# Token norms as a broadcast subtraction on VectorE and a broadcast product on GpSimd, and strided copies turned to strided reads

## The chip, the cores and the metric

The kernel runs on one core of a Trainium2 chip. A core has five engines that work side by side, each through its own instruction list in order: TensorE (PE, with its weight loads shown as PEld), VectorE (DVE), ScalarE (ACT), GpSimd (POOL) and SyncE (SP, which issues most DMAs). Matrix products are written to PSUM, a small memory of eight banks of 512 floats per partition; everything else lies in SBUF. GpSimd works on SBUF here, the other engines on both. The metric is the device time of one execution in microseconds (us). One execution was also recorded by the hardware profiler; all views below are of it.

## The reference

Two "metaformer" layers over x of shape [16, 128, 32, 32] (16 samples, 128 channels, 1024 positions, called tokens). Cut to what matters:

```python
# layer 0
x = x + linear_attention(layernorm_over_channels(x, eps=1e-6))   # group norm, q/k/v, softmaxes
t = tokens(x)                                                    # [16, 1024, 128]
t = t + stu(layernorm(t, eps=1e-5))                              # FFT convolution with 16 filters, 3 taps
x = image(t)
# layer 1
x = x + conv_block(layernorm_over_channels(x, eps=1e-6))         # 3x3 conv, bn, relu, 3x3 conv, bn, + , relu
t = tokens(x)
t = t + experts(layernorm(t, eps=1e-5))                          # 64 experts choose 8 tokens each of a sample
x = image(t)
```

Each of the four norms takes every token by itself: the mean and the variance over its 128 channels, then `(v - m) / sqrt(s + eps)`. These are the token norms of the title: 4 per sample, 64 in all.

## The kernel before

A sample is held as [128 channels x 1024 tokens], in eight tiles of 128 tokens (`NT = 8`). For a norm it is turned by eight transposes on PE (`transpose_in`, L128, or `transpose_in_classes`, L133, which takes the tokens q, q+8, q+16, ... as class q) into a PSUM tile `big` of two banks, [128 tokens x 8 x 128 channels]. ACT copies the tile to SBUF (`tok` L312, `ub` L416, `tok` L760, `tt` L791). `token_stats` reads PSUM: eight `bn_stats` (L95), then small operations on [128 x 8] (L99 to L105) on DVE that give the mean m, the sum q and the variance a (L103), and `rsqrt`, five small operations on POOL (L85 to L89), which gives r. The norm itself is done in eight pieces, one for each tile: in stage A by ACT (`token_norm_act`, L120, with the small helper nm = -m*r on DVE, L118), in stage C by DVE (`token_norm`, L111). Each piece is turned back by a transpose on PE (`transpose_out`, L138) into another `big`.

The stages, with the times of the profiled execution:

- A, 0 to about 487 us, `attention(b)` for 16 samples. The norm of `tok`; gt (L319 to L321), pg (L325, PE) and ga (L327, then rsqrt on POOL) for the group norm; xn (L335); the keys: matmul (L342), maximum ks (L349), broadcast subtraction ke (L350, DVE, PSUM to SBUF), exponential (L353, ACT), sum and reciprocal (L365, L366), broadcast product (L367, POOL, in place); the queries: matmul (L360), maximum (L362, DVE), exponential (L364, ACT), transposes (L128) and copy qt (L376), L377 and L378; the context cx (L385, L389), wy (L394, copied in L396), wt (L400, copied in L402); output py (L408) and the sum into x (L409). Then the norm of `ub`, the transposed copy u (L426), the spectra (matmuls L436 for two parities, values by L221 to L234, "butterflies" L252 to L268, POOL for the even parity and DVE for the odd one), the three-tap products (L453), their sum into x (L459) and its store (L460). `filters()` runs beside it: it loads 16 tiles mi (L469) and mixes them on DVE (L473, L475), and computes the spectra ph of the filters.
- G, about 487 to 787 us: filters made and multiplied (L528 to L590; copies with strided reads L541 and L543, contiguous ones L580 and L582). Nothing is changed here.
- C, about 787 to 1576 us, `convolve_and_route(b)`: inverse spectra (`classes`, on POOL and DVE, L701 to L728; matmul L749), sum into x (L754), norm of `tok`, copy into a padded image (L767), two convolutions (L666, 18 matmuls for each half), ACT and DVE between them (L771, L778, L781), sum into x (L783, POOL), norm of `tt`, transposes, copy tk (L799), gate product (L808), and for every second sample the choice of tokens (up to gt, L826), transposes of gt (L128, copy gtt L834) and the pooling pp (L840, copied in L845 and L849).
- the experts and the final sum, about 1576 to 1737 us. Nothing is changed here.

Samples overlap: `interleave` holds up to five samples of A (a new one every 4 steps) or four of C as generators, and at every `yield` goes on to the next one. A scheduling framework then orders the instructions of each engine and puts in the waits; each engine's order is fixed in the program. Tiles come from rings: `big` has three buffers in stage A and two in stage C, `tok` has three in A. A buffer is free again only when its last reader is done. So in A the centre of a loop is the chain L103 (DVE), rsqrt (POOL), norm, L138 (PE), and the two norms of different samples share DVE, POOL and the ring.

The strided copies: `ub` holds tokens by class, and `u` shall hold them in order. L426 read PSUM straight and wrote SBUF with a step of eight elements; L754 likewise wrote x, read and written with that step:

```python
nc.scalar.copy(
    u.rearrange("p (s q) -> p q s", q=NQ), pu.rearrange("p (q s) -> p q s", q=NQ)
)
```

The functions that the diff touches, with the line numbers of the profile:

Of the kernel before, what the change touches and what calls it, by code (L numbers as in the profile page):

```python
# [8 lines left out]
F32 = mybir.dt.float32  # L9
AF = mybir.ActivationFunctionType  # L10
ALU = mybir.AluOpType
# [3 lines left out]
P = 128  # L15
B, C, H, W = 16, 128, 32, 32
N = H * W
NT = N // 128
# [12 lines left out]
NQ = 8  # L31
# [24 lines left out]
def metaformer_kernel(ctx: ExitStack, tc: tile.TileContext, io: dict, out: bass.AP):  # L56
    nc = tc.nc
# [24 lines left out]
    def rsqrt(r, a, t):  # L82

        g = nc.gpsimd
        g.tensor_tensor(r, a, mhalf[:, : a.shape[1]], ALU.pow)  # L85
        g.tensor_tensor(t, r, r, ALU.mult)
        g.tensor_tensor(t, t, a, ALU.mult)
        g.tensor_scalar(t, t, -0.5, 1.5, ALU.mult, ALU.add)
        g.tensor_tensor(r, r, t, ALU.mult)  # L89

    def token_stats(work, src, eps):

        bst = work.tile([P, NT, 6], F32, name="bst", tag="bst")
        for j in range(NT):
            nc.vector.bn_stats(bst[:, j, :], src[:, j, :])  # L95
        sts = work.tile([P, 6, NT], F32, name="sts", tag="sts")
        m, q, r, d, a, t = (sts[:, i, :] for i in range(6))
        me, qe, mo, qo = (bst[:, :, i] for i in (1, 2, 4, 5))
        nc.vector.tensor_tensor(d, me, mo, ALU.subtract)  # L99
        nc.vector.tensor_tensor(q, qe, qo, ALU.add)  # L100
        nc.vector.tensor_tensor(d, d, d, ALU.mult)
        nc.vector.scalar_tensor_tensor(q, d, C / 4.0, q, ALU.mult, ALU.add)
        nc.vector.tensor_scalar(a, q, 1.0 / C, eps, ALU.mult, ALU.add)  # L103
        nc.vector.tensor_tensor(m, me, mo, ALU.add)
        nc.vector.tensor_scalar(m, m, 0.5, None, ALU.mult)  # L105
        rsqrt(r, a, t)
        return m, q, r

    def token_norm(dst, src, m, r):
        for j in range(NT):  # L110
            nc.vector.tensor_scalar(  # L111
                dst[:, j, :], src[:, j, :], m[:, j : j + 1], r[:, j : j + 1],
                ALU.subtract, ALU.mult,
            )

    def token_norm_act(work, dst, src, m, r):
        nm = work.tile([P, NT], F32, name="nm", tag="nm")
        nc.vector.scalar_tensor_tensor(nm, m, -1.0, r, ALU.mult, ALU.mult)  # L118
        for j in range(NT):
            nc.scalar.activation(  # L120
                dst[:, j, :], src[:, j, :], AF.Identity,
                bias=nm[:, j : j + 1], scale=r[:, j : j + 1],
            )

    def transpose_in(pt, src):

# [33 lines left out]
    with ExitStack() as l0:  # L160
# [42 lines left out]
        with ExitStack() as a0:  # L203
# [3 lines left out]
            work = a0.enter_context(tc.tile_pool(name="awork", bufs=2))  # L207
# [81 lines left out]
            for h in range(HEADS):  # L289
                s = slice(h * DH, (h + 1) * DH)  # L290
# [11 lines left out]
            def big():  # L302
                return ps.tile([P, N], F32, name="big", tag="big", bufs=3)

            def attention(b):
                if b + 2 < B:
                    load(b + 2)
                xb = xt[b]
                pt = big().rearrange("p (j c) -> p j c", c=C)
                transpose_in(pt, xb)  # L310
                tok = work.tile([P, NT, C], F32, name="tok", tag="tok", bufs=3)
                nc.scalar.copy(tok, pt)  # L312
                m, q, r = token_stats(work, pt, 1e-6)

                yield
                token_norm_act(work, tok, tok, m, r)

                gt = work.tile([P, NT + 1], F32, name="gt", tag="gt")
                nc.vector.scalar_tensor_tensor(gt[:, :NT], q, 1.0 / C, r, ALU.mult, ALU.mult)  # L319
# [12 lines left out]
                px = big()  # L332
# [40 lines left out]
                pt = big().rearrange("p (j c) -> p j c", c=C)  # L373
# [19 lines left out]
                pw = ps.tile([P, P], F32, name="pw", tag="s")  # L393
                nc.tensor.matmul(pw, cx, wout, start=True, stop=True)  # L394
                wy = work.tile([P, P], F32, name="wy", tag="wy")
                nc.vector.tensor_copy(wy, pw)  # L396

                yield
                pw = ps.tile([P, P], F32, name="pw", tag="s")
                nc.tensor.matmul(pw, wv, wy, start=True, stop=True)  # L400
                wt = work.tile([P, P], F32, name="wt", tag="wt")
                nc.vector.tensor_copy(wt, pw)  # L402

                yield
                py = big()
                for hf in range(2):
# [6 lines left out]
                pt = big().rearrange("p (j c) -> p j c", c=C)  # L413
                transpose_in_classes(pt, xb)
                ub = work.tile([P, NT, C], F32, name="ub", tag="ub")
                nc.scalar.copy(ub, pt)  # L416
                m, q, r = token_stats(work, pt, 1e-5)

                yield
                token_norm_act(work, ub, ub, m, r)  # L420

                yield
                pu = big()
                transpose_out(pu, ub)
                u = work.tile([P, N], F32, name="u", tag="u")
                nc.scalar.copy(  # L426
                    u.rearrange("p (s q) -> p q s", q=NQ), pu.rearrange("p (q s) -> p q s", q=NQ)
                )

                yield  # L430
# [31 lines left out]
            def filters():  # L462
# [34 lines left out]
                nc.vector.tensor_tensor(ph[:, :, half:], e, o, ALU.subtract)  # L497

            interleave(attention, 5, 4, filters())


# [114 lines left out]
    with ExitStack() as c1:  # L616
        cconst = c1.enter_context(tc.tile_pool(name="cconst", bufs=1))
        work = c1.enter_context(tc.tile_pool(name="cwork", bufs=2))
# [34 lines left out]
        for n in range(2):  # L653
            for i in range(2):
                pt = cconst.tile([P, HP, HP], F32, name=f"pad{n}{i}", tag=f"pad{n}{i}")
# [20 lines left out]
        def tokens(t):  # L676
            return t.rearrange("p (j c) -> p j c", c=C)
# [58 lines left out]
        def convolve_and_route(b):  # L736
            pr, j = divmod(b, 2)
# [4 lines left out]
            xb = xt[b]  # L742
# [3 lines left out]
            px = big()  # L746
            for q in range(NQ):
                for r in range(2):
# [1 line left out]
                        px[:, q * P : (q + 1) * P], z[:, q, r, :], wi[:, q, r, :],  # L750
                        start=(r == 0), stop=(r == 1),
                    )
            xv = xb.rearrange("p (s q) -> p q s", q=NQ)
            nc.vector.tensor_tensor(xv, px.rearrange("p (q s) -> p q s", q=NQ), xv, ALU.add)  # L754
            yield

            pt = tokens(big())
            transpose_in(pt, xb)
            tok = work.tile([P, NT, C], F32, name="tok", tag="tok")
            nc.scalar.copy(tok, pt)  # L760
            m, q, r = token_stats(work, pt, 1e-6)
            yield
            token_norm(tok, tok, m, r)
            yield
            px = big()
            transpose_out(px, tok)
# [8 lines left out]
            for hf in range(2):  # L775
                pc = conv(p2, cw[1], hf)
                r = work.tile([P, 16, W], F32, name="r", tag="r")
# [9 lines left out]
            pt = tokens(big())  # L787
            transpose_in(pt, xb)
            tt = work.tile([P, NT, C], F32, name="tt", tag="tt", bufs=4)
            toks[b] = tt  # L790
            nc.scalar.copy(tt, pt)  # L791
            m, q, r = token_stats(work, pt, 1e-5)
            yield
            token_norm(tt, tt, m, r)
            yield
            pu = big()
            transpose_out(pu, tt)
# [53 lines left out]
            )  # L851

        interleave(convolve_and_route, 4, 4)


# [5 lines left out]
    with ExitStack() as e1:  # L861
        work = e1.enter_context(tc.tile_pool(name="ework", bufs=2))
# [153 lines left out]
```

## Time and profile before

| what | us |
|---|---|
| three runs, median (lowest to highest) | 1737.72 (1735.78 to 1739.06) |
| the profiled execution | 1738.64 |
| its span | 1736.7 |
| PE busy, DVE busy | 1464.6, 883.2 |
| ACT busy, POOL busy | 583.6, 634.6 |
| rsqrt's first step on POOL, L85, 64 times | 108.6 |
| norm by ACT in stage A, L120, 256 pieces | 102.0 |
| norm by DVE in stage C, L111, 256 pieces | 68.4 |
| four kinds of ACT copies, 64 in all | 64.8 |
| u by L426, x by L754, 16 each | 32.2, 32.7 |

In the profile a group of instructions is written as line, engine, operation, output<-inputs by the program's names, and how many; then busy time in all, mean ns of one, and after the bar the idle time of that engine just before them, with what ended it. In a row of PE's waits, `PE big L138 <- DVE tt L111` is a transpose that stood until DVE had made tt; the numbers are us in total, times, and the longest. The chain of waits goes back from the last instruction: each piece is released by the one before it. L12 is line 12 of the kernel before.

### The profile page before, as it was taken

To read this page: it belongs to the slowest core of one execution; us is meant where nothing else is said; L and a number is where in the kernel's file an instruction comes from. 1 tells how busy PE (TensorE), PEld (TensorE's weight loads), DVE (VectorE), ACT (ScalarE), POOL (GpSimd) and SP (SyncE) were. 2 spreads that over 40 slices of the span, in tenths; PEclk is the share of its full clock that TensorE was granted. 3 is DMA by queue.
4 is the path that set the end of the run, shared out by engine and by line. 5 is a ranking of instruction groups with operands and counts; after the bars stand their busy time and mean duration, and the time that the engine had idled before them with its cause. 6 is when DMAs were issued, how large, how long until landed. Compare 5 with 4: busy or idle time off the path is not lost.

```text
span 1736.7 us, 32853 instructions
## 1 busy us (share of the span) xinstructions
PE 1464.6 (84%) x13704; PEld 943.4 (54%) x13704; DVE 883.2 (51%) x2509; ACT 583.6 (34%) x919; POOL 634.6 (37%) x926
## 2 busy tenths in 40 slices
PE   3688888888789999973999989999799979965675
PEld 2566666666568888862455444554455445432232
DVE  5676777767456666655345443533545253411114
ACT  3456655666345555540112221212112121211000
POOL 2354433444257777763333222331333133110000
PEclk9899999999889999995999989999899989986677
DMA  6311211211234444448101010110101000007965
GB/s 229 111 70 64 85 74 74 85 74 62 85 111 119 131 124 125 122 145 289 41 25 37 25 37 25 32 29 13 49 25 37 1 13 1 12 0 267 393 246 208
DMA packets 136420, 160.29 MB, mean 92 GB/s; under 512 B 4944, under 2 KB 104400, under 8 KB 133840
## 3 DMA queue, kind: packets, MB, share of 16 engines
q1 hardware_dynamic: 135504, 156.10, 26.4%
q8 instruction: 107, 1.75, 0.4%
q0 software_dynamic: 768, 2.10, 0.3%
q14 instruction: 41, 0.34, 0.1%
HBM read 102.61 MB, written 55.57 MB: 91 GB/s over the span
## 4 chain that ended last, share of the span: by engine, by line
PE 55%; DVE 14%; issue 11%; POOL 10%; ACT 4%; DMA 4%; SPq 2%; DVEq 0%; POOLq 0%; ACTq 0%
PE pcv L666 23%; PE pg L534 8%; PE py L554 8%; POOL sts L85 4%; PE big L749 3%; PE big L138 2%; DVE bst L95 2%; PE big L436 2%; PE big L128 2%; POOL ke L367 1%; POOL x L783 1%; PE pp L840 1%; PE big L808 1%; PE big L453 1%; ACT ub L120 1%
## 5 line engine op out<-in xcount | busy, mean ns | idle before, releaser
L666 PE MATMUL pcv<-pad,cw 128*128 128x512 f32 x1152 | 507.3, 595 | 0.7 <-ACT pad L767 0.7
L666 PEld LDWEIGHTS pcv<-pad,cw 128*128 128x128 f32 x1152 | 214.0, 190 | 259.6 <-issue 258.2
L85 POOL TENSOR_TENSOR sts<-sts,mhalf 128x8 f32<-128x8 f32 x64 | 108.6, 1697 | 296.5 <-DVE sts L103 296.5
L541 DVE COPY g<-pg 128x512 f32<-128x512 f32 x256 | 164.9, 686 | 97.4 <-PE pg L534 94.0
L543 ACT COPY g<-pg 128x512 f32<-128x512 f32 x256 | 137.5, 589 | 127.4 <-PE pg L534 118.9
L534 PE MATMUL pg<-ph,mst 32*128 32x128 f32 x4096 | 155.6, 287 | 6.1 <-ACT g L543 4.7
L95 DVE BATCH_NORM_STATS2 bst<-big 128x6 f32<-128x128 f32 x512 | 111.0, 280 | 77.4 <-ACT tt L791 61.4
L534 PEld LDWEIGHTS pg<-ph,mst 32*128 32x128 f32 x4096 | 131.0, 190 | 32.3 <-issue 25.2
L554 PE MATMUL py<-g,v 128*32 128x128 f32 x4096 | 140.3, 276 | 3.0 <-issue 2.3
L783 POOL TENSOR_TENSOR x<-x,r 128x512 f32<-128x512 f32 x32 | 40.5, 1265 | 258.7 <-ACT r L781 258.7
L554 PEld LDWEIGHTS py<-g,v 128*32 128x32 f32 x4096 | 105.5, 109 | 20.1 <-issue 5.4
L771 ACT ACTIVATE pad<-pcv,bn 128x512 f32<-128x512 f32 x32 | 25.0, 781 | 262.8 <-PE pcv L666 262.8
L523 POOL TENSOR_TENSOR v<-xc 128x512 f32<-128x512 f32 x64 | 80.6, 1287 | 47.1 <-PE py L554 29.6
L778 DVE SCALAR_TENSOR_TENSOR r<-pcv,bn,pad 128x512 f32<-128x512 f32 x32 | 24.0, 751 | 137.2 <-PE pcv L666 136.4
L453 PE MATMUL big<-u,mu 128*128 128x128 f32 (+4 forms) x384 | 92.2, 381 | 1.2 <-ACT u L426 1.2
L128 PE MATMUL big<-ident,x 128*128 128x128 f32 x384 | 56.7, 285 | 42.5 <-POOL x L783 23.0
L749 PE MATMUL big<-wi,z 128*128 128x128 f32 x512 | 70.3, 296 | 23.5 <-POOL z L703 21.2
L749 PEld LDWEIGHTS big<-wi,z 128*128 128x128 f32 x512 | 68.1, 211 | 29.9 <-POOL z L703 21.5
L436 PE MATMUL big<-wf,ub 128*128 128x256 f32 x256 | 67.4, 404 | 13.7 <-ACT u L426 7.8
L128 PEld LDWEIGHTS big<-ident,x 128*128 128x128 f32 x384 | 46.0, 146 | 55.6 <-POOL x L783 27.4
L781 ACT ACTIVATE r<-r,bn 128x512 f32<-128x512 f32 x32 | 23.1, 722 | 144.2 <-DVE r L778 144.0
L138 PE MATMUL big<-ident,tok 128*128 128x128 f32 x256 | 42.0, 299 | 34.3 <-DVE tok L111 17.9
(210 smaller groups left out, 2313.7 us busy)
## 6 DMA issues: line engine op xcount, KB each, us to landing
vd<-xf SPq DMA_DIRECT2D x16, 1024.0 KB, 3.8
xc<-vd SPq DMA_DIRECT2D x16, 1024.0 KB, 6.7
yd<-ys SPq DMA_DIRECT2D x32, 512.0 KB, 4.2
y<-yd SPq DMA_DIRECT2D x32, 512.0 KB, 5.5
w1t<-in_weight SPq DMA_DIRECT2D x16, 1024.0 KB, 14.7
w2t<-in_weight SPq DMA_DIRECT2D x16, 1024.0 KB, 14.4
x<-in_x SPq DMA_DIRECT2D x16, 512.0 KB, 3.5
mi<-in_M_phi SPq DMA_DIRECT2D x16, 512.0 KB, 3.9
```

The source lines that it names most:

```text
L85: g.tensor_tensor(r, a, mhalf[:, : a.shape[1]], ALU.pow)
L95: nc.vector.bn_stats(bst[:, j, :], src[:, j, :])
L128: nc.tensor.transpose(pt[:, j, :], src[:, j * P : (j + 1) * P], ident)
L436: lambda q, dst: nc.tensor.matmul(dst, ub[:, q, :], wf[:, q, :], start=True, stop=True),
L453: nc.tensor.matmul(pa[:, a:hi], mu[:, NF - 1 - si, tap, :], u[:, a - tap : hi - tap], start=(tap == 0), stop=(tap == KU - 1),)
L523: nc.gpsimd.tensor_tensor(vv[:, x, 1 + r], xc[:, :, 0, :, r, :], xc[:, :, 1, :, r, :], op)
L534: nc.tensor.matmul(pg[r][:, i], mst[rs, 4 * q + i, :], ph[rs, c, :], start=True, stop=True,)
L541: nc.vector.tensor_copy(dst, src)
L543: nc.scalar.copy(dst, src)
L554: nc.tensor.matmul(py[rows, x, kl, :], v[:, (x * NM + m) * JL + jl, 1 - ri : 3 - ri, :] .rearrange("p k b -> p (k b)"), g[:, ((x * NM + m) ...
L666: nc.tensor.matmul(pc, wt[:, tap, :], src[:, hf * 16 + dy : hf * 16 + dy + 16, dx : dx + W], start=(tap == 0), stop=(tap == 8),)
L749: nc.tensor.matmul(px[:, q * P : (q + 1) * P], z[:, q, r, :], wi[:, q, r, :], start=(r == 0), stop=(r == 1),)
```

## The change

The norm is split otherwise. `token_center` is one DVE operation on the whole tile: it reads PSUM, subtracts the mean (broadcast over the channels) and writes SBUF. It takes the place of ACT's copy and needs no r, and stands right behind `token_stats`. `token_scale` is one POOL operation, in place in SBUF, which multiplies by r (broadcast). It stands where the eight pieces stood; nm is gone. The copies of wy and wt go from DVE to ACT. The copies u and the sum L754 write SBUF in order and read PSUM with the step.

```diff
-    def token_norm(dst, src, m, r):
-        for j in range(NT):
-            nc.vector.tensor_scalar(
-                dst[:, j, :], src[:, j, :], m[:, j : j + 1], r[:, j : j + 1],
-                ALU.subtract, ALU.mult,
-            )
-
-    def token_norm_act(work, dst, src, m, r):
-        nm = work.tile([P, NT], F32, name="nm", tag="nm")
-        nc.vector.scalar_tensor_tensor(nm, m, -1.0, r, ALU.mult, ALU.mult)
-        for j in range(NT):
-            nc.scalar.activation(
-                dst[:, j, :], src[:, j, :], AF.Identity,
-                bias=nm[:, j : j + 1], scale=r[:, j : j + 1],
-            )
+    def token_center(dst, src, m):
+        nc.vector.tensor_tensor(
+            dst, src, m.unsqueeze(2).to_broadcast([P, NT, C]), ALU.subtract
+        )
+
+    def token_scale(dst, r):
+        nc.gpsimd.tensor_tensor(dst, dst, r.unsqueeze(2).to_broadcast([P, NT, C]), ALU.mult)
...
                 tok = work.tile([P, NT, C], F32, name="tok", tag="tok", bufs=3)
-                nc.scalar.copy(tok, pt)
                 m, q, r = token_stats(work, pt, 1e-6)
-
-                yield
-                token_norm_act(work, tok, tok, m, r)
+                token_center(tok, pt, m)
+
+                yield
+                token_scale(tok, r)
...
-                nc.vector.tensor_copy(wy, pw)
+                nc.scalar.copy(wy, pw)
...
-                nc.vector.tensor_copy(wt, pw)
+                nc.scalar.copy(wt, pw)
...
                 ub = work.tile([P, NT, C], F32, name="ub", tag="ub")
-                nc.scalar.copy(ub, pt)
                 m, q, r = token_stats(work, pt, 1e-5)
-
-                yield
-                token_norm_act(work, ub, ub, m, r)
+                token_center(ub, pt, m)
+
+                yield
+                token_scale(ub, r)
...
                 nc.scalar.copy(
-                    u.rearrange("p (s q) -> p q s", q=NQ), pu.rearrange("p (q s) -> p q s", q=NQ)
+                    u.rearrange("p (s q) -> p s q", q=NQ), pu.rearrange("p (q s) -> p s q", q=NQ)
                 )
...
-            xv = xb.rearrange("p (s q) -> p q s", q=NQ)
-            nc.vector.tensor_tensor(xv, px.rearrange("p (q s) -> p q s", q=NQ), xv, ALU.add)
+            xv = xb.rearrange("p (s q) -> p s q", q=NQ)
+            nc.vector.tensor_tensor(xv, px.rearrange("p (q s) -> p s q", q=NQ), xv, ALU.add)
...
             tok = work.tile([P, NT, C], F32, name="tok", tag="tok")
-            nc.scalar.copy(tok, pt)
             m, q, r = token_stats(work, pt, 1e-6)
-            yield
-            token_norm(tok, tok, m, r)
+            token_center(tok, pt, m)
+            yield
+            token_scale(tok, r)
...
-            nc.scalar.copy(tt, pt)
             m, q, r = token_stats(work, pt, 1e-5)
-            yield
-            token_norm(tt, tt, m, r)
+            token_center(tt, pt, m)
+            yield
+            token_scale(tt, r)
```

## The prediction

> **What bounds the kernel now.** I read the page first: no engine is full over the whole span, so the share of busy time decides nothing, and each stage has to be read for itself.
>
> ```profile
> span 1736.7 us, 32853 instructions
> PE 1464.6 (84%) x13704; PEld 943.4 (54%) x13704; DVE 883.2 (51%) x2509; ACT 583.6 (34%) x919; POOL 634.6 (37%) x926
> ```
>
> The change touches stage A (0 to 487 us) and stage C (787 to 1576 us). One steady sample of A, in the table by windows, takes 25.45 us (the distance of two L409):
>
> ```profile
> 311.93:337.38 25.45, 22.41 (x127) 16.51 (x127) 18.64 (x62) 16.35 (x29) 11.59 (x23) 1.00 0.21 84
> ```
>
> The columns after the length are PE, its weight loads, DVE, ACT and POOL. PE lacks 3 us, DVE 6.8, POOL 13.9: no engine sets the pace. The chain of waits in the same stretch shows what does, a loop through DVE, POOL and back:
>
> ```profile
> 322.60 0.17 DVE sts L103
> ...
> 322.89 1.66 POOL sts L85
> ...
> 325.96 0.89 ACT ub L120 x2
> ...
> 329.68 1.91 POOL ke L367
> 331.59 1.61 POOL sts L85
> ...
> 334.11 0.21 POOL sts L89
> ...
> 336.02 1.28 DVE x L409
> ```
>
> The reader should see that POOL is on the chain although it is idle more than half of the time. In stage C, PE is full with the convolution (L666) but for three stretches where one group of samples ends and the next begins; the waits of PE in that stage (total us, times, longest) name them:
>
> ```profile
> PE big L128 <- POOL x L783: 23.0, 15, 2.5
> PE big L138 <- DVE tt L111: 19.5, 4, 7.0
> PE big L138 <- DVE tok L111: 17.9, 4, 10.5
> PE big L128 <- issue: 9.0, 3, 3.0
> ```
>
> **The prices.** From the groups of instructions:
>
> ```profile
> L350 DVE TENSOR_TENSOR ke<-big,ks 128x1024 f32<-128x1024 f32 x16 | 19.4, 1212 | 0.0
> L367 POOL TENSOR_TENSOR ke<-ke,ks 128x1024 f32<-128x1024 f32 x16 | 31.0, 1939 | 71.4 <-PE big L138 36.1 <-DVE sts L103 20.5 <-DVE qs L377 12.7
> L120 ACT ACTIVATE ub<-ub,nm,sts 128x128 f32<-128x128 f32 x128 | 51.0, 480 | 35.4 <-DVE nm L118 35.4
> L111 DVE TENSOR_SCALAR tok<-tok,sts 128x128 f32<-128x128 f32 x128 | 34.2, 340 | 43.4 <-POOL sts L89 43.4
> L426 ACT COPY u<-big 128x1024 f32<-128x1024 f32 x16 | 32.2, 2010 | 9.2 <-PE big L138 9.2
> L754 DVE TENSOR_TENSOR x<-big,x 128x1024 f32<-128x1024 f32 x16 | 32.7, 2043 | 70.4 <-PE big L749 70.4
> L799 ACT COPY tk<-big 128x1024 f32<-128x1024 f32 x16 | 16.2, 1014 | 31.4 <-PE big L138 31.1
> L95 DVE BATCH_NORM_STATS2 bst<-big 128x6 f32<-128x128 f32 x512 | 111.0, 280 | 77.4 <-ACT tt L791 61.4
> ```
>
> Centre: L350 is the same operation in form (PSUM in, SBUF out, small factor broadcast): 1.21 us. Scale: L367 likewise, 1.91 as median and 2.36 at worst, when DVE worked beside it; I take 1.95. The old norm was eight pieces, 3.19 us on ACT or 2.14 on DVE, the first done after 0.5 or 0.36; the new scale releases all eight transposes (L138) together. Copies of the strided u (L426) and sum (L754) keep the strided side, but read it from PSUM. No row strides over two PSUM banks; within one bank the strided reads L541 and L543 (686 and 589 ns) equal the contiguous L580 and L582 (681 and 586). So u is between 1.01 (L799) and 2.01, L754 between 1.21 and 2.04, and I take the lower values, the nearest rows.
>
> [...]
>
> **Stage A, steady.** Removed per sample: two ACT copies (L312, L416, 1.01 each), 16 activations (L120), two nm (L118), two DVE copies that go to ACT (L396, L402, 0.28 each; about the same there, on an engine with 9 us to spare, so they cost nothing; if ACT were late they would add 0.3 each ahead of L400 and L408). Added: two centres (2.4 on DVE), two scales (3.9 on POOL). ACT falls to some 9 us, DVE rises by 1.5 to about 20, POOL to 15.5. All still fit in 25.4. The loop does not stay, because order changes on two engines:
>
> - On DVE the centre of ub stands ahead of L103, whose output POOL waits for. Before, L103 ended at 322.76; now at 323.87.
> - On POOL: rsqrt (2.9) to 326.8, scale of ub (1.95) to 328.75, L367 to 330.7, rsqrt of tok (2.8) to 333.5. Before it was 334.32: from L103 the leg is 9.63 instead of 11.56, since the tok statistics no longer queue on DVE behind L118. L367 is not later than its other input, L366, allows.
> - After that rsqrt, DVE executes L319 to L321 (0.45) and only then L362, the maximum of q (1.2), in 10 of 16 samples; before, L362 stood ahead of the wait and was over by 331.7. Then L364 on ACT (1.3), L408 (1.9; its PSUM buffer is the one that L364 reads), L409 (1.3): end 339.75. This leg is 6.25 instead of 3.0. Behind L362 on DVE wait L459, L377 and L409.
> - From L409 to the next L103: 10.9 before. The centre adds 1.2, the copies and nm take 0.25 away, and L436's odd half starts some 0.55 before L409's end instead of 0.06 behind it (its buffer comes free with L234): 11.25.
>
> Sum 9.63 + 6.25 + 11.25 = 27.1; with the PE stalls before L138 (328.75 against 326.5 for the first piece before), partly made good by u's missing 1.0 us, I take 27.0 to 27.3, +1.7 per sample. On PE, L325 (for ga) now comes after all eight transposes of tok instead of among them: nothing, since xn (L335) needs those transposes as well. On SP's queue two loads of mi (L469) come earlier, between loads of x; each 512 KB load lands in about 4 us and DMA engines are 21% busy here: nothing, and 4 us once if a load of x stood behind them. Bounds: if what stands behind L362 is not late, 26.4 (+1.0), less what PE's slack takes back (+0.6); with matmul ends as listed 28.1 (+2.7). About ten such periods lie between 118 and 412 us: **+17** (+6 to +28).
>
> Fill (0 to 118 us): xn of the first sample waits for the ga chain, which the change does not shorten: 0 (-3 to +3).
>
> Drain (412 to 487 us): here samples no longer overlap. In the last one L103 goes ahead of the centre. Before, rsqrt ended 470.52, the eight pieces and transposes ran to 476.3, u was copied until 478.75. Now the scale ends at 472.8, eight transposes in a row at 475.0 (0.27 each at that place), u at 476.05: -2.7. Two samples before it gain about 0.7 each by u: **-4** (-6 to 0; 0 with u at 2.01).
>
> **Stage C.** Per sample go two ACT copies and 16 L111, and come two centres and two scales. PE is full in most of it, so DVE's and POOL's new work is covered by L666 (7.7 us per 18 matmuls); POOL's L783 wait shows what it costs if the scale falls ahead of L783: up to 1.95 a time. I price that at nothing since L783 is ready when L781 is, a few us after the scales.
>
> At the three boundaries: L95 of tt waits for no copy (-1.0), L754 is 0.8 shorter, and the tok statistics no longer stand behind L111 and L845, which waited for 31 matmuls (L840, to 1042.66). Their L103 falls at about 1037.75 instead of 1043.43; rsqrt to 1041.4 (behind the scale of tt, POOL first), scale to 1043.4, transposes from 1043.5 to 1045.2, pad and first L666 at about 1046.5 where it was 1051.63; less 0.6 for L749 that now follow in one block: -4.5 each, **-13.5** (-18 to -4). Start of C: one copy and L754 less, a centre and an unsplit scale more: 0 (-1 to +1). In the steady part, at some four places a transpose of the next tile needs the PSUM buffer that the centre now holds 0.85 longer than the copy did: **+3.5** (0 to +7). End of C: centre ahead of L103 and the eight cold transposes behind the scale, one copy less: **+1.5** (0 to +3).
>
> Sum: +17 - 4 - 13.5 + 3.5 + 1.5 = +4.5. The profiled execution took 1738.64 us (span 1736.7 and 1.9 around it), 0.9 above the median of the three runs, 1737.72. So about 1742.
>
> **Rivals.**
> 1. *The loop of A is not stretched, faster.* If L362's delay is taken by the depth of five samples in flight (PSUM ring of three buffers, PE with 3 us of slack) and the removed copies free DVE early, A adds at most 0.6 a sample: +6 - 4 - 13.5 + 3.5 + 1.5 = -6.5; with no stretch at all -12.5. Time 1725 to 1732. Against it: the order of DVE puts L362 behind a wait for POOL. It decides where the period stays under 26.2.
> 2. *POOL sets the pace, much slower.* POOL works 15.5 of 25.4 us, all of it in the chain. With scale and L367 at 2.36, and L252 to L257 (the spectra's even half) queued between them, the period goes to 28 and over: +27, boundaries then only -3 each: +20, about 1758.
> 3. *The strided read costs what the strided write did.* u and L754 stay at 2.0: drain 0, boundaries -3.7 each, period +0.5 more: about +15, 1753. The change then only moves the stride. The contiguous-equal rows L541 and L580 speak against it.
>
> **How the numbers follow.** Forecast 0.43 (its own range 1734 to 1751), rival 1 0.32, rival 2 0.17, rival 3 0.08. Within 0.2% (3.5 us, about what a measurement of this kernel can tell from no change) lie 0.13 of the forecast's chance and 0.03 of rival 1; below it 0.04 and 0.29; the rest above. Faster 0.33, same 0.16, slower 0.51. The range reaches to 1722 (rival 1 with the boundaries' full bound) and 1764 (rival 2 with the contention at its worst row), leaving out about 0.2.
>
> **What would show it.** Right: windows between L409 of 27 us in steady A; PE waiting for POOL's scale before L138; L362 behind L319 with ACT waiting at L364; boundaries of C 4 us shorter; u near 1.0 and L754 near 1.2. Wrong: a steady window of 25.5 or less (rival 1), a scale over 2.3 with DVE beside it (rival 2), u at 2.0 (rival 3). The sum is most exposed to the number of stretched periods, and to PE's order, where eight L138 in a row now wait at one place with L453 and L436 behind them.

## The result and the profile after

The changed kernel takes 1789.43 us (median of 4 runs, 1785.93 to 1791.74) against 1737.73 us of the kernel before beside it: 1.0297 times, 95% interval 1.0275 to 1.0318. That is 2.97% slower, 51.7 us, where +4 was forecast and the range ended at 1764. In the profiled execution the span is 1786.2 us, 49.5 more than before. The page of the changed kernel:

```profile
span 1786.2 us, 32455 instructions
PE 1467.9 (82%) x13704; PEld 952.3 (53%) x13704; DVE 895.0 (50%) x2253; ACT 414.9 (23%) x631; POOL 750.3 (42%) x990
```

ACT lost 169 us of work, POOL gained 116, DVE 12, and PE has the same work. In the changed kernel the line numbers are 8 lower from stage A on (L401 is the old L409, L354 the old L362, L400 the old L408, L445 the old L453, L658 the old L666); L110 is the centre, L115 the scale, L130 the transposes L138. Where the 49.5 us lie, from the first and last instruction of one line in each stage:

| stretch | before | after | difference | forecast |
|---|---|---|---|---|
| A, fill: to the third sum of py into x (L409, now L401) | 118.2 | 127.7 | +9.5 | 0 |
| A, steady: from the third to the fourteenth | 294.1 | 337.7 | +43.6 | +17 |
| A, drain: to the first product of G | 73.4 | 74.2 | +0.8 | -4 |
| G: its first to its last pg | 277.9 | 279.2 | +1.3 | 0 |
| start of C: to the first convolution product | 57.0 | 57.9 | +0.9 | 0 |
| C: first to last convolution product | 721.7 | 712.5 | -9.2 | -13.5 + 3.5 |
| the rest | 194.4 | 197.0 | +2.6 | +1.5 |

Stage C came out nearly as forecast. Stage A is the miss, and within it the steady part: one sample takes 30.7 us instead of 25.4. The table by windows (as in the prediction: length, then PE, weight loads, DVE, ACT, POOL, granted clock, DMA) of one steady sample, and below it three parts of the same sample:

```profile
374.64:405.32 30.68, 23.31 (x127) 17.21 (x127) 22.36 (x61) 7.69 (x12) 15.15 (x25) 0.94 0.18 68
385.50:395.80 10.30, 8.18 (x37) 5.27 (x38) 6.86 (x21) 2.07 (x2) 8.65 (x12) 1.00 0.01 2
395.80:400.40 4.60, 1.84 (x9) 1.28 (x7) 4.36 (x5) 1.22 (x3) 1.92 (x2) 0.98 0.00 0
400.44:404.00 3.56, 3.56 (x6) 1.56 (x7) 1.58 (x4) 0.42 (x1) 2.33 (x5) 0.55 0.41 158
```

No engine is full here either, but two things are new. From 395.8 to 400.4 PE works only 1.84 us of 4.6 while DVE is busy, and in the stretch behind it PE's granted clock is 0.55. The timeline of this sample (start, us, engine, line, operation; in brackets the idle time before it and what ended it) names both, and the delay of L99 before them:

```profile
388.27 1.20 DVE L357 TENSOR_REDUCE ks<-ke 128x32 f32<-128x1024 f32 x1
388.58 1.90 POOL L115 TENSOR_TENSOR ub<-ub,sts 128x1024 f32<-128x1024 f32 x1
389.39 1.11 DVE L99 TENSOR_TENSOR sts<-bst 128x8 f32<-128x8 f32 x1
...
395.90 1.90 POOL L115 TENSOR_TENSOR tok<-tok,sts 128x1024 f32<-128x1024 f32 x1
396.06 1.76 DVE L312 TENSOR_TENSOR gt<-gt,sts 128x8 f32<-128x8 f32 x1
397.86 0.16 DVE L313 TENSOR_REDUCE gt<-gt 128x1 f32<-128x8 f32 x1
397.93 1.21 DVE L354 TENSOR_REDUCE qs<-big 128x1 f32<-128x1024 f32 x1
...
400.44 3.56 PE L400 MATMUL big<-xn,wt 128*128 128x512 f32 x4 [2.80 <-ACT qe L356]
```

In the steady sample of the kernel before, L312 (there L320) and L400 (there L408) read:

```profile
333.53 1.88 PE L408 MATMUL big<-xn,wt 128*128 128x512 f32 x4
335.64 0.15 DVE L320 TENSOR_TENSOR gt<-gt,sts 128x8 f32<-128x8 f32 x1
```

L312 works on 128x8 numbers and took 0.155 us on average before. Now it takes 1.76 in ten of the 16 samples, this one among them, and ends at 397.82, just after POOL's scale of tok (395.90 + 1.90 = 397.80). L99 ends at 390.50, just after the scale of ub (390.48). Neither shows idle time before it: the delay hides as length. Then L354, L356 and L400 follow late, PE has stood 2.80 us, and four products that took 1.88 before, at a granted clock of 1.00, take 3.56 at 0.55.

### The profile page after: what moved, and what is told of

Same layout as the page of the kernel before. It is cut to its first block, busy times and chain, and to the rows that moved or that the text cites. A ratio compares the mean times of both kernels' runs of the same rounds, so it can differ in the third digit from the quotient of the medians.

```text
span 1786.2 us, 32455 instructions
## 1 busy us (share of the span) xinstructions
PE 1467.9 (82%) x13704; PEld 952.3 (53%) x13704; DVE 895.0 (50%) x2253; ACT 414.9 (23%) x631; POOL 750.3 (42%) x990
## 3 DMA queue, kind: packets, MB, share of 16 engines
q1 hardware_dynamic: 135504, 156.10, 25.6%
## 4 chain that ended last, share of the span: by engine, by line
PE 58%; DVE 13%; issue 11%; POOL 10%; DMA 4%; ACT 3%; SPq 1%; DVEq 0%; POOLq 0%; ACTq 0%
PE pcv L658 23%; PE pg L526 8%; PE py L546 7%; PE big L741 3%; POOL sts L85 2%; PE big L130 2%; PE big L120 2%; PE big L400 2%; DVE bst L95 2%; PE big L428 2%; PE big L334 2%; PE big L800 1%; POOL ke L359 1%; POOL x L775 1%; PE pc L377 1%
## 5 line engine op out<-in xcount | busy, mean ns | idle before, releaser
L658 PE MATMUL pcv<-pad,cw 128*128 128x512 f32 x1152 | 506.5, 594 | 0.7 <-ACT pad L759 0.7
L658 PEld LDWEIGHTS pcv<-pad,cw 128*128 128x128 f32 x1152 | 213.3, 189 | 259.2 <-issue 258.1
L445 PE MATMUL big<-u,mu 128*128 128x128 f32 (+4 forms) x384 | 95.0, 394 | 16.5 <-DVE ub L110 16.5
L741 PE MATMUL big<-wi,z 128*128 128x128 f32 x512 | 64.9, 285 | 24.3 <-POOL z L695 21.8
L741 PEld LDWEIGHTS big<-wi,z 128*128 128x128 f32 x512 | 63.2, 200 | 31.3 <-POOL z L695 22.0
L445 PEld LDWEIGHTS big<-u,mu 128*128 128x128 f32 x384 | 57.1, 195 | 35.9 <-DVE ub L110 18.7
L746 DVE TENSOR_TENSOR x<-big,x 128x1024 f32<-128x1024 f32 x16 | 19.6, 1225 | 111.0 <-PE big L741 110.7
L120 PEld LDWEIGHTS big<-ident,x 128*128 128x128 f32 x384 | 45.1, 145 | 50.2 <-POOL x L775 27.5
L896 POOL DMA_DIRECT2D ed<-og x16 | 8.7, 546 | 137.7 <-DVE og L895 137.7
```

What stands on the lines that cost most here:

```text
L120: nc.tensor.transpose(pt[:, j, :], src[:, j * P : (j + 1) * P], ident)
L445: nc.tensor.matmul(pa[:, a:hi], mu[:, NF - 1 - si, tap, :], u[:, a - tap : hi - tap], start=(tap == 0), stop=(tap == KU - 1),)
L658: nc.tensor.matmul(pc, wt[:, tap, :], src[:, hf * 16 + dy : hf * 16 + dy + 16, dx : dx + W], start=(tap == 0), stop=(tap == 8),)
L741: nc.tensor.matmul(px[:, q * P : (q + 1) * P], z[:, q, r, :], wi[:, q, r, :], start=(r == 0), stop=(r == 1),)
```

## Theories and experiments

Theory 1: DVE operations on SBUF alone stand while POOL's scale runs; L312 delays L354, and PE's idle time then halves its clock. Rival 2: POOL's chain of rsqrt, scale and product sets the period, and L312 only lies beside it. Rival 3: L312 is slow because it shares the operand r with the scale. Later a fourth came in: a second loop through the centre and the scale of ub. (These rivals are not those of the prediction.) Each run below is given as its median time and its ratio to the kernel before, run beside it, with the 95% interval.

**The delayed operation: its kind.** First L312 with one tensor input:

```diff
-nc.vector.scalar_tensor_tensor(gt[:, :NT], q, 1.0 / C, r, ALU.mult, ALU.mult)
-nc.vector.tensor_tensor(gt[:, :NT], gt[:, :NT], r, ALU.mult)
+nc.vector.tensor_scalar(gt[:, :NT], r, 1.0 / C, None, ALU.mult)
+nc.vector.tensor_scalar(gt[:, :NT], gt[:, :NT], 1.0, None, ALU.mult)
```

> The changed kernel; L311 and L312 on DVE become operations with one tensor input (r, then gt), at the same place in every engine's order and with the same wait for r; what they compute (the weight of a token in the group norm) is left out. Theory 1 (DVE operations with two SBUF inputs stand while POOL works on its scale): L312 falls from 1.76 to about 0.16 us though it still reads while the scale runs, and PE's idle time before L400 shrinks by 1.6 us; if PE's lowered clock at L400 (0.55 granted) follows from that idle time, L400 x4 falls from 3.56 to 1.9 as well. A steady period goes from 30.7 to 29.1 without and 27.4 with the clock's part; times 11 that is 1772 or 1753 us. Rival 2 (POOL's chain of rsqrt, scale, product sets the period, L312 is only beside it): 1789, unchanged. Rival 3 (L312 is slow because it shares the operand r with the scale): L312 stays at 1.76, 1789.

Measured: 1786.64 us, 1.0291 (1.026 to 1.0322), steady period 30.7. The timeline of this kernel:

```profile
393.98 1.90 POOL L115 TENSOR_TENSOR tok<-tok,sts 128x1024 f32<-128x1024 f32 x1
394.14 1.76 DVE L312 TENSOR_SCALAR gt<-gt 128x8 f32<-128x8 f32 x1
```

L312 stands as long as before, now with one input and without r. So rival 3 falls, and theory 1 in the form "two inputs" as well. Taken alone, the unchanged time would have spoken for rival 2; that L312 was not relieved shows that the run had not tested it. The next run changes the kind of operation only:

```diff
-nc.vector.tensor_tensor(gt[:, :NT], gt[:, :NT], r, ALU.mult)
+nc.vector.tensor_reduce(gt[:, :NT], gt[:, :NT].unsqueeze(2), AX.X, ALU.add)
```

> The changed kernel; only L312 on DVE becomes a reduction over one element (output as input; the second factor r of the group norm's weight is left out), at the same place in every engine's order, still behind the same wait for r. In the run with a one-input TENSOR_SCALAR at L312 it stayed at 1.76 us and the time at 1787. Theory 1a (what is kept from running beside POOL's product is the kind of DVE operation: two SBUF inputs or a copy-like one from SBUF to SBUF, but not a reduction): L312 takes 0.16, a steady period falls from 30.7 to 29.1, and to 27.4 if PE's low clock at L400 came from the idle time that L312 causes; times 11: 1771 or 1753 us. Rival (any small SBUF operation of DVE stands while POOL's scale runs, or the period is set elsewhere): L312 1.76 or the time at 1787.

Measured: 1760.26 us, 1.012 (1.0103 to 1.0136): 29 us of the 52 are gone by the kind of one operation on 1024 numbers in each sample, at the same place in the order and behind the same waits. Its timeline and the window of L400:

```profile
379.39 1.90 POOL L115 TENSOR_TENSOR tok<-tok,sts 128x1024 f32<-128x1024 f32 x1
379.54 0.16 DVE L312 TENSOR_REDUCE gt<-gt 128x8 f32<-128x8 f32 x1
...
382.32 1.98 PE L400 MATMUL big<-xn,wt 128*128 128x512 f32 x4 [1.19 <-ACT qe L356]
```

```profile
382.32:384.30 1.98, 1.98 (x6) 0.97 (x7) 1.59 (x4) 0.42 (x1) 0.75 (x2) 1.00 0.64 265
```

The reduction runs beside the scale in 0.16 us, PE stands 1.19 us instead of 2.80, keeps its clock (1.00), and the steady period is 27.5. Theory 1a holds: 1.6 us of delay and 1.6 us of clock in each of the eight samples where PE had stood 2.8 us make 25.6, and A ends 26.8 us earlier (512.8 instead of 539.6).

By kind, beside the scale's 1.90 us: 1.76 us for the TENSOR_TENSOR, with two inputs, 1.76 for the TENSOR_SCALAR, with one, and 0.16 for the reduction. What ties the delay to the instruction's kind no run here shows; "locked" and "lock" in the expectations below are the author's words for an operation that stands like this.

**For how long.** The scale of tok in two halves:

```diff
-token_scale(tok, r)
+for hf in range(2): token_scale(tok[:, 4 * hf : 4 * hf + 4], r[:, 4 * hf : 4 * hf + 4])
```

> The changed kernel; tok's scale in stage A is issued as two operations of 512 elements on POOL. If POOL holds what DVE needs for the length of one instruction, L312 waits for the first half only: about 0.8 to 0.9 us instead of 1.76. If it holds it as long as any POOL work is queued: 1.8 as before.

Measured: 1771.95 us in one run. L312 takes 0.88 to 0.91 in twelve of 16 samples: it waits for one instruction, the first half, and is over at 385.10 while the second half runs until 386.07 (2.04 us for both). From two steady samples of this kernel:

```profile
384.03 2.04 POOL L115 TENSOR_TENSOR tok<-tok,sts 128x512 f32<-128x512 f32 x2
384.19 0.91 DVE L312 TENSOR_TENSOR gt<-gt,sts 128x8 f32<-128x8 f32 x1
...
387.71 3.52 PE L400 MATMUL big<-xn,wt 128*128 128x512 f32 x4 [1.93 <-ACT qe L356]
...
447.56 1.98 PE L400 MATMUL big<-xn,wt 128*128 128x512 f32 x4 [0.24 <-ACT qe L356]
```

The run adds a middle point for the clock. With PE idle for 2.8 us before it, L400 took 3.44 to 3.68 us in all eight samples of the changed kernel; with 1.93 us it took 1.98, 2.75, 2.94, 3.08 and 3.52; with 1.2 or less, in these two kernels, 1.88 to 1.98 (and 1.98 in two early samples with 1.8 and 2.1). The idle time alone does not decide: in the run with gt as 1 - eps/a, below, L400 took 1.98 in an early sample behind 2.62 us. In all traces here the granted clock changes only on a grid of 3.41 us. On that grid the sample of the changed kernel reads, in the table by windows:

```profile
396.82:400.23 3.41, 0.82 (x4) 0.38 (x2) 3.38 (x4) 1.05 (x2) 0.98 (x1) 1.00 0.00 0
400.23:403.65 3.42, 3.21 (x4) 1.40 (x5) 1.66 (x5) 0.63 (x3) 1.98 (x4) 0.50 0.37 153
403.65:407.06 3.41, 3.41 (x23) 3.01 (x22) 1.35 (x2) 1.16 (x2) 2.35 (x8) 1.00 0.52 154
```

PE was busy for 0.24 of the first window, and the second has half the clock. Over all 14 traces, between 100 and 480 us, each of the 63 windows at full clock (1.00) in which PE was busy for less than 0.41 of the time was followed by one at half clock (0.50), and none of the 1333 with more than 0.52; of the 54 between, 29 were. In the kernel before these are 3, 100 and 2 windows, with one half clock behind the 2; in the changed kernel 10, 86 and 4, with none behind the 4. The changed kernel's period of 30.7 us is nine such windows, so its eight samples met the grid at nearly the same place and are not eight independent trials.

A window did not have to be idle for that: 0.82 us of work in the first row above, and whatever lay below 0.41, went ahead of half clock.

**The other delayed operation.** L99, L100 and L104 as reductions too:

```diff
-nc.vector.tensor_tensor(d, me, mo, ALU.subtract)
-nc.vector.tensor_tensor(q, qe, qo, ALU.add)
+nc.vector.tensor_reduce(d, bst[:, :, 1::3], AX.X, ALU.subtract)
+nc.vector.tensor_reduce(q, bst[:, :, 2::3], AX.X, ALU.add)
...
-nc.vector.tensor_tensor(m, me, mo, ALU.add)
+nc.vector.tensor_reduce(m, bst[:, :, 1::3], AX.X, ALU.add)
```

> The same, and L99, L100 and L104 (differences and sums of the half-tile statistics) become reductions over two elements, in the same order on every engine. L99 stood about 1.0 us in each steady period until POOL's scale of ub ended. Theory 1a: L99 takes 0.16 and the period falls by another 0.65 us (L367's successor L359 on POOL can start only when the scale ends): 7 us less than the run with L312 alone. Rival: L99's delay lies beside POOL's own work, no change against that run.

Measured: 1762.43 us, 1.0135 (1.0118 to 1.0152). L99 takes 0.16 throughout, but the period is 27.3 or 27.9 instead of 27.5 and the time is no lower. The delay of L99 was real and beside the path. The expected 7 us are not there.

**The order on DVE.** What is left is 27.5 against 25.4, about what the prediction had put on the order of L354 behind the wait for r. First gt from the variance, as 1 - eps/a, which needs no r:

```diff
-nc.vector.scalar_tensor_tensor(gt[:, :NT], q, 1.0 / C, r, ALU.mult, ALU.mult)
-nc.vector.tensor_tensor(gt[:, :NT], gt[:, :NT], r, ALU.mult)
+nc.vector.reciprocal(gt[:, :NT], a)
+nc.vector.tensor_scalar(gt[:, :NT], gt[:, :NT], -1e-6, 1.0, ALU.mult, ALU.add)
```

> The changed kernel; gt is computed as 1 - eps/a from the variance a (a reciprocal and one scalar operation, both with one tensor input), so that DVE no longer waits for POOL's rsqrt before L354. Theory (order on DVE: L354 queues behind a wait for POOL, then behind the locked L312, then PE's clock is low): all three go, the leg from rsqrt's end to L401's end falls from 9.5 to about 5 or less, period 25.5 to 26.5 with only the locked L99 (1.0) and the centre ahead of L103 (1.2) left; about 1736 to 1750 us. Rival 2 (POOL's chain sets the pace): period stays over 29, 1775 or more.

Measured: 1760.23 us, 1.0124 (1.0104 to 1.0145), period 26.3 or 28.0. L312 still stood 0.61 us in many samples. So a run without that:

```diff
-nc.vector.tensor_scalar(gt[:, :NT], gt[:, :NT], -1e-6, 1.0, ALU.mult, ALU.add)
+nc.vector.tensor_reduce(gt[:, :NT], gt[:, :NT].unsqueeze(2), AX.X, ALU.add)
```

> The changed kernel; L311 to L313 take the variance a instead of r and are a reciprocal and two reductions (the group norm's weight is left out in part), so DVE neither waits for POOL's rsqrt ahead of L354 nor stands while POOL's scale runs. With the delay at L312 alone taken away the period was 27.5 us. If the order on DVE (L354 behind a wait for r) is what stretches those 27.5 from the 25.4 of before, the period falls to 25.4 to 26.3 and the time by 13 to 25 us, to 1735 to 1747. If a second loop is as long (centre ahead of L103, rsqrt, scale of ub in one piece, transposes L130, which PE then does at its low clock): period 26.3 to 28 and 1752 to 1760.

Measured: 1760.35 us, 1.0133 (1.011 to 1.0156), period still 26.3 or 28.0. The wait for r is gone, PE no longer stands before L400, and nothing is gained against 1760.26: a second loop is as long. The chain of waits in that kernel shows it:

```profile
365.59 1.23 DVE ks L341
366.82 0.07 DVE sts L102
366.89 1.14 DVE ub L110
368.02 0.09 DVE sts L103
...
368.18 1.66 POOL sts L85
...
371.05 1.91 POOL ub L115
372.95 0.04 issue
373.00 1.09 PE big L130 x8
374.09 3.39 PE big L445 x4
```

The centre (1.14) stands on the chain ahead of L103, then come rsqrt and the whole scale (1.91), PE stands 2.02 us before L130, whose eight take 1.09 at a granted clock of 0.96, and the four products L445 behind them take 3.39 at 0.51. The last run makes the mean of every norm depend on the variance, so that L103 comes first (C's length from first to last convolution product does not change by it, 711.9):

```diff
-nc.vector.tensor_scalar(m, m, 0.5, None, ALU.mult)
+nc.vector.scalar_tensor_tensor(m, m, 0.5, a, ALU.mult, ALU.bypass)
```

> The same, and the mean m is made to depend on the variance, so that L103 stands ahead of the centre of ub (and of L342) on DVE and POOL can begin its rsqrt 1.2 to 2.4 us earlier. If the second loop (centre, rsqrt, scale, L130) sets the period then: 1.2 us or more less per period than the run without it, 10 to 15 us in all. If not: no change (within 3 us), or slower, since the centre and with it the PSUM buffer for L445 come later.

Measured: 1732.67 us, 0.9967 (0.9953 to 0.9982): 27.7 us less, twice what was expected. Period 25.35, stage A ends at 485.6 us as in the kernel before (485.7). The same chain:

```profile
348.41 0.07 DVE sts L102
348.48 0.21 DVE bst L95
348.69 0.08 DVE sts L103
...
351.71 1.91 POOL ub L115
353.61 0.04 issue
353.66 1.09 PE big L130 x8
354.75 1.72 PE big L445 x4
```

The centre's 1.14 us have left the chain (0.21 of a bn_stats is in its place), PE stands 0.75 us before L130 instead of 2.02, and L445 takes 1.72 at a granted clock of 1.00. Against this kernel's 25.35, the clock cost 1.7 of the 2.6 us in the periods of 28.0, the order 0.9; in those of 26.3 (L445 x4 in 1.88 behind the same 2.01 us of idle time) the order alone. POOL's scale is still in one piece in this kernel, so rival 2 falls: POOL does as much as in the changed kernel and the period is that of before.

**Scale on ACT.** Eight pieces on ACT in stage A (for tok as for ub), and gt as 1 - eps/a:

```diff
+def token_scale_act(dst, r):
+    for j in range(NT):
+        nc.scalar.activation(dst[:, j, :], dst[:, j, :], AF.Identity, scale=r[:, j : j + 1])
...
-token_scale(ub, r)
+token_scale_act(ub, r)
```

> Stage C as in the changed kernel. In stage A the centre stays on DVE, the scale goes to ACT in eight pieces (no POOL scale, nothing that DVE's small operations could wait for), and gt comes from the variance, without a wait for POOL. DVE's order has L103 ahead of the centre and L354 ahead of gt. If the lock, the order and the clock are all of A's loss: A ends at 485 us or earlier, period 25.4 or less, 1722 to 1735 us. If a DVE centre in A costs by itself (it holds the PSUM buffer longer than the copy): period 26 to 27, 1740 to 1755.

Measured: 1737.29 us, 1.0 (0.9982 to 1.0019), period 26.1: the time lies between the two expected ranges, the period in the second. The expectation had L103 ahead of the centre, but in this kernel's chain the centre of ub (1.14 us from 353.41) still stands ahead of L103, and the period is close to the 26.3 that the run without the wait shows where L445 x4 took 1.88 and not 3.39. So the run does not show that a centre costs by itself. The third sum of py into x (L405 here) is at 120.0 (127.7 in the changed kernel, 118.2 before): without POOL's scale most of the fill's loss is gone. As the order and gt differ too, the run does not separate the causes of those 9.5 us; in the run above, with the scale on POOL, the third was at 122.3.

**Stage C alone**, with stage A as before; in the changed kernel's code:

```diff
-token_center(tok, pt, m)
+nc.scalar.copy(tok, pt)
...
-token_scale(tok, r)
+token_norm_act(work, tok, tok, m, r)
```

(in A only, the same for ub; wy, wt and u as before too.)

> Stage A as before the change, stage C as after it. If the loss is all in A: the part from the first to the last convolution matmul falls from 721.2 to about 712 us as in the changed kernel, and the time to about 1729 us (1726 to 1733). If C's gain in the changed kernel came from the state that A leaves behind (clock, loads): 1738.

Measured: 1733.09 us, 0.9963 (0.9945 to 0.998). First to last convolution product 711.9 us: the gain in C is its own. The three stretches without a convolution product are 3.3, 3.7 and 3.8 us shorter than before, and the parts before, between and behind them are within 0.8 us of before. Behind the last convolution product 2.4 us are lost again, and the time is just above what was expected.

The same, with u read by the step (the edit stands below) and gt as 1 - eps/a in A (of its two lines the second is shown):

```diff
-nc.vector.tensor_tensor(gt[:, :NT], gt[:, :NT], r, ALU.mult)
+nc.vector.tensor_scalar(gt[:, :NT], gt[:, :NT], -1e-6, 1.0, ALU.mult, ALU.add)
```

> Stage C as after; stage A as before but with u read with the step from PSUM and written in order, and gt computed from the variance a. u takes 1.0 instead of 2.0 us and is waited for by L436 in 13 of 16 samples: up to 1 us less per period, 0 to 16 us in A; C -9. About 1720 us (1712 to 1730). If A's loop does not contain u: 1729.

Measured: 1733.19 us, 0.9968 (0.9955 to 0.9981); u took the shorter time, but the period is 25.67. With u alone:

```diff
 nc.scalar.copy(
-    u.rearrange("p (s q) -> p q s", q=NQ), pu.rearrange("p (q s) -> p q s", q=NQ)
+    u.rearrange("p (s q) -> p s q", q=NQ), pu.rearrange("p (q s) -> p s q", q=NQ)
 )
```

> Stage C as in the changed kernel; stage A as before it, only that u (L426 of the kernel before) is read with the step from PSUM and written in order: 1.01 instead of 2.01 us, 16 times. If u lies on A's loop, the period falls from 25.4 to 24.5 and A by some 10 us: 1723. If not (in the run that also took gt from the variance the period was 25.67): A's end at 484 to 486 us and the time within 2 us of the 1733 us of stage C alone.

Measured: 1729.81 us, 0.9954 (0.994 to 0.9969). u takes 1010 ns, the period stays at 25.43, A ends at 483.5 instead of 486.2: u is on the path only where samples no longer overlap. This version is faster than both kernels, by 0.46% against the kernel before; its interval overlaps that of stage C alone.

Last, C's scale in eight pieces on ACT instead of one on POOL, with A as before:

```diff
-token_scale(tt, r)
+token_scale_act(tt, r)
```

> Stage A as before the change. In stage C the centre is on DVE, the scale on ACT in eight pieces instead of on POOL in one. ACT works a quarter of C, and the first transpose can start 0.4 us after r instead of 1.9: if the unsplit scale costs that at the three group boundaries and at the end of C, first to last convolution matmul takes 706 to 709 instead of 712 us, the end of C 1.5 less, the time 1724 to 1729 us. If the boundaries are set by DVE (L103 behind the class sums, which wait for POOL): 1731 to 1735.

Measured: 1734.7 us, 0.9987 (0.9966 to 1.0008); first to last convolution product 715.7 us, 3.7 more than with POOL's scale. At each of the three boundaries PE's transposes L150 (L138 before the change) waited there behind another copy of ACT, gtt, which ACT begins only when its eight pieces are done, as PE's waits show:

```profile
PE big L150 <- ACT gtt L846: 10.2, 3, 3.4
```

So the run shows that eight pieces on ACT are no gain there, and not what the unsplit scale costs on POOL: in the changed kernel that scale stands in the chain of the first boundary with 1.91 us (from 1092.52).

## Why the prediction was wrong

**Prices.** The centre measured 1218 ns (1.21 taken), the scale 1900 (1.95), u 1013 (1.01), L754 as L746 1225 (1.21). All are right, and rival 3 of the prediction, that the strided read costs what the strided write did, falls on these rows:

```profile
L115 POOL TENSOR_TENSOR tok<-tok,sts 128x1024 f32<-128x1024 f32 x32 | 60.8, 1900 | 2.5
L418 ACT COPY u<-big 128x1024 f32<-128x1024 f32 x16 | 16.2, 1013 | 72.6 <-PE big L130 72.6
L746 DVE TENSOR_TENSOR x<-big,x 128x1024 f32<-128x1024 f32 x16 | 19.6, 1225 | 111.0 <-PE big L741 110.7
```

**The step that failed** is the second leg of the steady loop: "After that rsqrt, DVE executes L319 to L321 (0.45)", then L362, L364, "L408 (1.9 ...)", 6.25 in all. The leg measured 9.5: L319 to L321 took 2.1 (the middle one stood 1.76, until the scale ended), and L408 3.56 at a granted clock of 0.55. The other legs were 10.2 (9.63 forecast) and 11.0 (11.25). In the kernel with L312 as a reduction the second leg is 6.3 and the period 27.5, beside 27.1 worked out: the mechanism of the order was right, and two terms, +1.6 and +1.7, were missing. (Two sums of the prediction are slightly off: the terms listed for this leg make 6.15, and those of its rival 2 make +19 and not +20.) The prediction considered contention only in one direction, as POOL's operations made longer by DVE (2.36 at worst). The other direction could be read in the kernel before, at a boundary of C, where POOL works on the class sums; in its chain of waits:

```profile
1030.31 0.41 DVE sts L99
1030.72 0.68 DVE sts L100
1031.40 0.41 DVE sts L104
```

These small operations take 0.08 in the steady sample of A. It was there that a price had to be looked for, since the change puts 64 scales of 1.9 us beside just these operations. Stage A of the kernel before even held the price itself, once among the 32 nm, whose median is 0.17 us, beside a product of the scale's shape:

```profile
255.25 1.91 POOL L367 TENSOR_TENSOR ke<-ke,ks 128x1024 f32<-128x1024 f32 x1
255.33 1.85 DVE L118 SCALAR_TENSOR_TENSOR nm<-sts 128x8 f32<-128x8 f32 x1 [0.30 <-POOL sts L89]
```

**Bounds and the prediction's rivals.** The upper bound of a period, 28.1, had no term for a clock below 1.00, as no row of the steady sample before had one. Rival 2 named a period of 28 and over, with POOL as the pace; its size was nearer than its reason. Rival 1 (no stretch) was wrong; in no run that kept L354 behind the wait for r did the samples in flight absorb the delay.

**What the order is worth.** The forecast put the stretch on L354 behind the wait for r. The run without that wait shows a second loop of the same length, in which the forecast's first point (the centre ahead of L103) decides. With both gone the period fell to 25.35; no run took away the second alone. The prediction had summed the two in one loop.

**Fill and drain.** 0 and -4 were forecast, +9.5 and +0.8 measured. In the drain u's gain shows where it is alone (A ends about 2.7 us earlier, with A as before but for u); in the changed kernel the drain is no shorter in all, and what took the gain away no run shows. The fill was priced by xn of the first sample, which ended 1.5 us later (29.9 instead of 28.4). Of the 9.5 us, 4.3 lie ahead of the first sum of py into x, 4.5 between the first and the second, and 0.7 ahead of the third; which waits make them up stays open.

**Stage C.** -9.2 from first to last convolution product where the terms made -10. The stretches at the boundaries are 3.1, 3.7 and 3.8 us shorter and not 4.5 each: L103 of tt still came late, behind L716, which waits for POOL's class sums. The delay of DVE is there too: beside the scale of tt (from 1092.52) L101 of the next norm stood 1.88 us. The steady parts between cost 1.3 together where 3.5 was put. The last norm, from the last convolution product to the last pooled transpose, takes 34.0 instead of 32.7 us: +1.3, as forecast (+1.5); its eight transposes, cold in the prediction's word, took 2.18 us before and 1.97 after, both at a granted clock of 0.50.

G's 1.3 us stay unexplained; its code is the same in all kernels, and its length in the runs above lay between 275 and 282 us.

## What to carry to other kernels

Before a large elementwise operation moves to GpSimd, list the small VectorE operations on SBUF that will run beside it, by kind (here 1.76 us for a TENSOR_TENSOR and 0.16 for a reduction), and look in the old profile for rows where the same line takes several times its usual length while GpSimd works. Price a new wait of PE twice, once as time and once as what PE's clock will be behind it (here 2.80 us, and 3.56 instead of 1.88 for the four products that followed). When one loop is cut and the time stays, look for a second loop of the same length before giving up the first explanation.

## What was not expected of the hardware

A VectorE TENSOR_SCALAR on 128x8 numbers in SBUF stood 1.76 us beside GpSimd's 1.90 us product, a TENSOR_REDUCE of the same size 0.16, and the profile shows the delay as busy time, not as a wait. On a grid of 3.41 us, PE's granted clock was halved in the step behind each of the 63 steps at full clock in which PE was busy for less than 0.41 of the time, and behind none above 0.52 (100 to 480 us, all traces). With a step of eight elements on the side that writes SBUF, ACT's copy took 2010 ns and DVE's sum, which also read SBUF with it, 2043; with a step of 128 elements on the side that reads PSUM they take 1013 and 1225.
